# A decoder on one core: FFN, latent text, first preparation and maxima as one list of single steps

## The chip, the cores and the metric

The kernel runs on one core of a Trainium2 chip. The time is the device time of one execution in microseconds (us), lower is better. Three runs of the kernel before took 1716.5, 1719.92 and 1722.71, median 1719.92. All data are float32 unless a line says otherwise.

## What is computed

Six residual blocks run one after another on x of 2 batches x 1024 rows x 256 features:

```python
x = x + linear_attention_and_ffn(layernorm(x))   # stage 1
x = x + latent_cross_attention(ctx, layernorm(x), mask)   # stage 2
x = x + gated_recurrence(layernorm(x))
x = x + causal_attention(layernorm(x))
x = x + cross_attention(layernorm(x), ctx)
x = x + experts(layernorm(x))
```

The change touches stage 1 and the beginning of stage 2:

```python
# stage 1, four heads of 64; b = batch
h = layer_norm(x, ln1)
q = softmax(h @ wq * scale, over 64 features); k = softmax(h @ wk * scale, over rows)
h0 = x + q @ (k.T @ (h @ wv)) @ wo + bo
y = h0 + gelu(layer_norm(h0, ln2) @ w_ff1 + b_ff1) @ w_ff2 + b_ff2
x_out = y @ w_d + b_d
# stage 2, four heads of 64; 64 text keys and the 1024 rows themselves
xn, ln = layernorm(ctx), layernorm(layernorm(x))
q, k, v = ln @ Wq.T, concat(xn, ln) @ Wkv.T ...
out = softmax(mask(rmsnorm(q) * gq / 8 @ rmsnorm(k).T * gk)) @ v @ Wo.T + bo
```

## The kernel before, in words

x stays in SBUF as 16 tiles of 128 rows. Stage 1 works on groups of four tiles (512 rows): groups 0 and 1 are batch 0, groups 2 and 3 batch 1. Stage 2 works by batch; a "unit" is a batch and a pair of heads (units 0 to 3).

Each engine carries out its own instructions strictly in the order in which the program issues them, and waits on semaphores for what other engines produce. Around the change the order is written by hand (`manual_schedule`): the order of the steps in the program is the order of every engine's queue.

**Stage 1** (class Linear, lines 246 to 632) consists of named steps with one engine each. `stat`, `mean`, `norm`, `h0_` are DVE, `root` a power on POOL, `turn` four transposes of 128 x 128 on TensorE into a ps_t tile, `hT` the copy out of it (feature half 0 on DVE, half 1 on ScalarE). `key`, `val`, `query` are eight products each into a ps_s tile; `kmax`, `kneg`, `kexp` and `qmax` to `qdiv` the two softmaxes. `ctx`, `cbd`, `wc`, `wcs` fold k.T v and wo into one matrix per batch; `att`, `radd` add the result to h0. For each group then follow `fstat` to `fT` (second layer norm and turn), eight `up` (two products of 128 x 512 into a ps_t tile) with `gelu` (ScalarE), four `down` (four products into the ps_f tile), `res` (adds h0 by eight products with the identity), `oT` (ScalarE), `last` (eight products into a ps_f tile), `bd` and `ladd` (DVE, into x).

`LINEAR_ORDER` (line 226) lists these steps for the attention of both batches and the FFN of groups 0 and 1, up to the turns of groups 2 and 3. The FFN of groups 2 and 3 is the generator `back` (line 615).

**Stage 2** (class Latent, from line 635) has `text` (line 692), which reads and projects the 128 text rows in few long steps, and `prepare` (line 773), which for one batch takes statistics, a doubled layer norm with two powers on POOL (L144, called from lines 787 and 792), transposes (L808), query-key products in four pieces (L822), squares and copies (ScalarE), sums (L834), a power on POOL (L836), values (L846), scaling (L857) and the transposes of q and k of both head pairs (L867, copied on ScalarE at L870). `start` interleaves `text` and `prepare(0)`; line 2549 interleaves `start` and the two `back` generators, one piece of each in turn.

`maxima(u)` (line 876) finds the largest score of each row of a unit in 18 steps: two text blocks (L886, reduced at L895 and L898) and 16 blocks of 128 rows x 512 keys x 2 heads (L908, reduced by DVE at L915), then a few small DVE operations that split the maxima in three bfloat16 parts (L918 to L925). `augment(u)` turns these for the attention. In `run` (line 1065) all 18 steps of unit 0 and four of unit 1 (LEAD) are issued first, then `attend(0)` follows, with one further max step of unit 1 and one piece of `prepare(1)` per loop step.

PSUM has eight banks. During stage 1 and line 2549 they are two ps_s tiles of two banks, two ps_t tiles of one bank and one ps_f tile of two (`ps_a`, line 2520). From `run` on there are three ps_s tiles, one ps_t and one ps_o (`ps_d`, line 2555). A tile is only written again when its readers are done.

Of the kernel before, what the change touches and what calls it, by code (L numbers as in the profile page):

```python
# [225 lines left out]
LINEAR_ORDER = """  # L226
stat_0 mean_0 stat_1 root_0 mean_1 norm_0 root_1 h0_0 turn_00 turn_01 hT_01 hT_00 norm_1 stat_2 turn_11
turn_10 hT_11 hT_10 h0_1 key_00 stat_3 mean_3 query_00 kmax_00 root_3 kneg_00 mean_2 kexp_00 h0_3 root_2
val_00 qmax_00 qsub_00 bd_0 qexp_00 key_01 vcopy_00 norm_2 qsum_00 qinv_00 qdiv_00 turn_21 turn_20 hT_21
kmax_01 val_01 hT_20 kneg_01 bd_1 kexp_01 kinv_0 qturn_001 norm_3 vcopy_01 qturn_000 qT_001 kturn_00  # L230
qT_000 kturn_01 kr_00 turn_30 kr_01 h0_2 turn_31 query_01 hT_31 hT_30 key_10 qmax_01 qsub_01 qexp_01
ctx_0 qsum_01 qinv_01 qdiv_01 kmax_10 qturn_010 query_10 qT_010 kneg_10 cbd_0 kexp_10 wc_0 qmax_10
qturn_011 wcs_0 val_10 qT_011 qsub_10 qexp_10 qsum_10 att_01 vcopy_10 qinv_10 qdiv_10 qturn_100 radd_01
qturn_101 att_00 qT_101 qT_100 fstat_1 fmean_1 froot_1 key_11 radd_00 fnorm_1 fstat_0 fturn_11 val_11
fmean_0 fT_11 kmax_11 froot_0 kneg_11 fnorm_0 kexp_11 kinv_1 fturn_00 vcopy_11 kturn_10 fT_00 fturn_01
kr_10 kturn_11 fT_01 up_01 kr_11 up_03 gelu_01 up_05 gelu_03 up_02 gelu_05 up_07 gelu_02 up_04 gelu_07
up_00 gelu_04 up_06 gelu_00 down_00 gelu_06 fturn_10 query_11 fT_10 up_12 qmax_11 qsub_11 up_13 gelu_12
qexp_11 down_01 gelu_13 qsum_11 qinv_11 qdiv_11 qturn_111 up_15 qT_111 down_02 gelu_15 up_11 down_03
gelu_11 res_0 up_17 oT_0 up_10 gelu_17 up_16 gelu_10 down_10 gelu_16 down_11 qturn_110 up_14 qT_110
ctx_1 gelu_14 down_12 cbd_1 wc_1 down_13 wcs_1 att_11 res_1 radd_11 fstat_3 att_10 oT_1 fmean_3 froot_3  # L240
fnorm_3 last_1 radd_10 fstat_2 fmean_2 fturn_31 ladd_1 froot_2 fturn_30 fT_31 fT_30 last_0 fnorm_2
fturn_21 ladd_0 fturn_20 fT_21 fT_20
"""


class Linear:
# [355 lines left out]
    def attention(self, own):  # L602

        self.own = own
        self.ksum = own.tile([P, B, DC], F32, tag="ksum", bufs=1, name="ksum")
        self.blocks = []
        for b in range(B):
            c = own.tile([P, DC, P], F32, tag=f"cbd{b}", bufs=1, name=f"cbd{b}")
            self.k.nc.gpsimd.memset(c, 0.0)
            self.blocks.append(c)  # L610
        for step in LINEAR_ORDER.split():
            name, args = step.rsplit("_", 1)
            getattr(self, "h0_" if name == "h0" else name)(*(int(a) for a in args))

    def back(self, g):

        for f2 in range(4):
            for fc in (2 * f2, 2 * f2 + 1):
                self.up(g, fc)
                self.gelu(g, fc)  # L620
            yield
            if f2:
                self.down(g, f2 - 1)
                yield
        self.down(g, 3)
        yield
        self.res(g)
        self.oT(g)
        yield
        self.bd(g)  # L630
        self.last(g)
        self.ladd(g)


class Latent:
# [13 lines left out]
    def __init__(self, k, x, wt, pool):  # L649
# [40 lines left out]
        self.undivided = None  # L690

    def text(self, ctx, mask):

        k, nc, pool, w = self.k, self.k.nc, self.pool, self.w
        tile = lambda name, shape, dt=F32: pool.tile(shape, dt, tag=name, bufs=1, name=name)
        cr = tile("cr", [P, CK])
        nc.sync.dma_start(out=cr, in_=ctx)

        m8 = tile("m8", [P, B * CTX], U8)
        nc.sync.dma_start(out=m8, in_=mask[0].partition_broadcast(P))  # L700
        self.mrow = tile("mrow", [P, B, CTX])
        nc.vector.tensor_copy(self.mrow.rearrange("p b n -> p (b n)"), m8)
        nc.vector.tensor_scalar(self.mrow, self.mrow, 1.0, -NEG, ALU.subtract, ALU.mult)
        c8 = tile("c8", [P, B], U8)
        for hh in range(2):
            for b in range(B):
                nc.sync.dma_start(
                    out=c8[hh * 64 : hh * 64 + 64, b : b + 1],
                    in_=mask[0, b * CTX : (b + 1) * CTX].unsqueeze(1),
                )  # L710
        self.mcol = tile("mcol", [P, B])
        nc.vector.tensor_copy(self.mcol, c8)
        nc.vector.tensor_scalar(self.mcol, self.mcol, 1.0, -NEG, ALU.subtract, ALU.mult)
        self.kbd = tile("kbd", [P, B, 2, 2, CTX])
        self.vbd = tile("vbd", [P, B, 2, 2, 64])
        nc.gpsimd.memset(self.kbd, 0.0)
        nc.gpsimd.memset(self.vbd, 0.0)
        mv, r = k.ln_stats(lambda i: cr, 1)
        nc.vector.tensor_scalar(cr, cr, mv[:, 0, 0:1], r[:, 0:1], ALU.subtract, ALU.mult)
        yield  # L720
        tb = k.t()
        for kc in range(2):
            nc.tensor.transpose(tb[:CP, kc * P : (kc + 1) * P], cr[:, kc * CP : (kc + 1) * CP], k.ident)

        xcT = tile("xcT", [CP, 2, B, 2, CTX])
        for kc in range(2):
            for d in range(2):
                k.affine(
                    xcT[:, kc, :, d, :],
                    tb[:CP, kc * P : (kc + 1) * P].rearrange("p (b n) -> p b n", b=B),  # L730
                    k.vec("ln_x_g", kc, CP), k.vec("ln_x_b", kc, CP), d,
                )
        yield
        for b in range(B):
            tb = k.t()
            for kc in range(2):
                nc.tensor.matmul(
                    tb,
                    lhsT=xcT[:, kc, b].rearrange("p d n -> p (d n)"),
                    rhs=w["ckv"][:CP, kc, :],  # L740
                    start=(kc == 0),
                    stop=(kc == 1),
                )
            kt = pool.tile([P, D], F32, tag="ckt", bufs=2, name="ckt")
            sq = pool.tile([P, D], F32, tag="cksq", bufs=2, name="cksq")
            nc.scalar.copy(kt, tb[:, :D])
            for hh in range(2):
                sl = slice(hh * 64, hh * 64 + 64)
                nc.vector.tensor_copy(
                    self.vbd[sl, b, :, hh, :],  # L750
                    tb[sl, D:].rearrange("p (r h d) -> p r h d", h=2, d=64)[:, :, hh, :],
                )
            yield
            nc.vector.tensor_mul(sq, kt, kt)
            ss = k.small([P, 4], "ss4")
            nc.vector.tensor_reduce(ss, sq.rearrange("p (h d) -> p h d", d=64), AX.X, ALU.add)
            nc.vector.tensor_scalar(ss, ss, 1.0 / 64, 1e-16, ALU.mult, ALU.max)
            ri = k.rsqrt(ss, 4)
            k3 = kt.rearrange("p (h d) -> p h d", d=64)
            nc.vector.tensor_tensor(k3, k3, ri.unsqueeze(2).to_broadcast([P, 4, 64]), ALU.mult)  # L760
            tb = k.t()
            for pr in range(2):
                nc.tensor.transpose(tb[:, pr * P : (pr + 1) * P], kt[:, pr * P : (pr + 1) * P], k.ident)
            for hh in range(2):
                sl = slice(hh * 64, hh * 64 + 64)
                nc.vector.tensor_scalar_mul(
                    self.kbd[sl, b, :, hh, :],
                    tb[sl, : 2 * P].rearrange("p (r d n) -> p r d n", r=2, d=2)[:, :, hh, :],
                    self.gk[sl],
                )  # L770
            yield

    def prepare(self, b):

        k, nc, pool, x, w = self.k, self.k.nc, self.pool, self.x, self.w
        lnT = pool.tile([P, DC, N], F32, tag="lnT", bufs=1, name="lnT")

        st, mv = k.small([P, TB, 6], "pr_st", 1), k.small([P, TB, 2], "pr_mv", 1)
        u, rr, nm = (k.small([P, TB], f"pr_{n}", 1) for n in ("u", "rr", "nm"))
        for i in range(TB):  # L780
            nc.vector.bn_stats(st[:, i, :], x[:, 8 * b + i, :])
            if i == 3:
                yield
        for i in range(TB):
            nc.vector.bn_aggr(mv[:, i, :], st[:, i, :])
        nc.vector.tensor_scalar_add(u, mv[:, :, 1], EPS)
        r = k.rsqrt(u, TB)
        yield
        nc.vector.tensor_mul(u, r, r)
        nc.vector.tensor_mul(u, u, mv[:, :, 1])  # L790
        nc.vector.tensor_scalar_add(u, u, EPS)
        r2 = k.rsqrt(u, TB)
        yield
        nc.vector.tensor_mul(rr, r2, r)
# [262 lines left out]
    def start(self, ctx, mask):  # L1057
# [4 lines left out]
        for _ in zip_longest(prepare, text):  # L1062
            yield
# [1620 lines left out]
```

## Time and profile before

The profiled execution took 1725.12 us, of which the span from the first to the last instruction is 1723.4; the other three runs have a median of 1719.92.

| stretch (us from the start) | what runs | TensorE busy | DVE busy | granted TensorE clock |
|---|---|---|---|---|
| 0 to 50 | loads, attention | 39.06 | 40.28 | 1.00 |
| 50 to 100 | attention, FFN | 50.00 | 22.60 | 1.00 |
| 100 to 150 | FFN of groups 0 and 1 | 49.05 | 8.68 | 1.00 |
| 150 to 200 | FFN of group 2, text, batch 0 | 39.37 | 24.37 | 0.90 |
| 200 to 250 | FFN, preparation of batch 0 | 50.00 | 18.66 | 1.00 |
| 250 to 275 | FFN of group 3 | 24.52 | 3.44 | 1.00 |
| 275 to 300 | maxima of unit 0 | 22.51 | 24.69 | 1.00 |
| 300 to 400 | attention of unit 0, preparation of batch 1 | 94.43 | 56.62 | 0.98 |

A busy time is the union of an engine's instructions in the stretch. The end of a matmul in the trace is modelled, so a TensorE that waits a little between two blocks still counts as busy. The clock is the share of full speed that the throttle granted. Products of float32 leave two records each in the trace.

### The profile page before, as it was taken

Reading aid. Unit: us, or ns where it says so; the run is one execution under the profiler, and the core shown is the slowest. Engines: PE = TensorE matmul, PEld = TensorE weight load, DVE = VectorE, ACT = ScalarE, POOL = GpSimd, SP = SyncE. Lnnn points to the kernel's source line nnn. Section 1 sums busy time; section 2 is a strip of 40 time slices with the busy share of each in tenths; the row PEclk is TensorE's granted clock in tenths of the full one; section 3 lists DMA queues with packets and bytes.
Section 4 is the critical chain, followed back from the end, with each engine's and each line's share of the span. In section 5 each row is a group of like instructions: output and inputs, shape, how many; then the busy total and the mean of one; then the engine's idle time right before and its main releaser. Section 6 shows DMA issues by size and latency. Waiting matters only on the chain.

```text
span 1723.4 us, 21309 instructions
## 1 busy us (share of the span) xinstructions
PE 1647.6 (96%) x8815; PEld 885.6 (51%) x8822; DVE 804.0 (47%) x1454; ACT 522.5 (30%) x876; POOL 319.6 (19%) x376
## 2 busy tenths in 40 slices
PE   7998899999999999999999999989999999999998
PEld 5746454343433447443433443446785664666466
DVE  8514236646654425476676668376531311111322
ACT  2321231432223323235455455423221111111110
POOL 2001140342222301113111011220035000000520
PEclk9999999999999999979999999989899999999999
DMA  5000000000000100100000000080014322232321
GB/s 232 1 1 3 1 0 0 1 1 1 1 1 1 40 1 1 32 1 2 1 2 1 1 1 1 2 273 2 1 68 164 122 84 66 95 122 72 106 64 49
DMA packets 36824, 69.68 MB, mean 40 GB/s; under 512 B 5048, under 2 KB 28152, under 8 KB 36344
## 3 DMA queue, kind: packets, MB, share of 16 engines
q1 hardware_dynamic: 28712, 53.61, 9.3%
q0 software_dynamic: 4608, 11.54, 2.1%
q10 hardware_dynamic: 3408, 3.17, 0.5%
q8 instruction: 70, 1.15, 0.3%
q14 instruction: 26, 0.21, 0.0%
HBM read 54.15 MB, written 14.16 MB: 40 GB/s over the span
## 4 chain that ended last, share of the span: by engine, by line
PE 80%; DVE 11%; issue 5%; ACT 2%; POOL 1%; DMA 0%; ACTq 0%; POOLq 0%; DVEq 0%
PE ps_s L2407 18%; PE ps_o L2434 9%; PE ps_s L1396 8%; PE ps_o L1436 5%; PE ps_s L1020 4%; PE ps_t L1355 4%; PE ps_o L947 3%; PE ps_t L1201 3%; PE ps_t L1471 2%; PE ps_s L908 2%; PE ps_t L539 2%; PE ps_s L822 2%; PE ps_s L381 2%; DVE part L915 1%; PE ps_f L556 1%
## 5 line engine op out<-in xcount | busy, mean ns | idle before, releaser
L2407 PE MATMUL ps_s<-xe,w 128*128 128x512 f32 (+1 forms) x528 | 229.0, 592 | 0.0
L1506 ACT ACTIVATE pT<-ps_t 128x512 f32<-128x512 f32 (+3 forms) x344 | 150.6, 490 | 150.3 <-PE ps_t L1471 148.9
L1396 PE MATMUL ps_s<-kT,qT 32*128 32x512 f32 (+3 forms) x768 | 182.9, 574 | 10.0 <-DVE part L1412 6.2
L1471 PE MATMUL ps_t<-qT,kT 32*128 32x512 f32 (+3 forms) x688 | 185.6, 557 | 2.2 <-ACT pT L1506 2.2
L2422 DVE TENSOR_TENSOR hid<-ga,ps_s 128x512 f32<-128x512 f32 (+2 forms) x99 | 62.0, 628 | 266.4 <-ACT ga L2418 266.3
L2407 PEld LDWEIGHTS ps_s<-xe,w 128*128 128x128 f32 (+1 forms) x528 | 98.0, 187 | 121.3 <-issue 120.0
L2434 PE MATMUL ps_o<-wo,hid 128*128 128x256 f32 (+1 forms) x704 | 153.7, 379 | 0.0
L1412 DVE TENSOR_REDUCE part<-ps_s 128x2 f32<-128x1024 f32 (+3 forms) x128 | 130.6, 1024 | 46.9 <-PE ps_t L1471 38.8
L2434 PEld LDWEIGHTS ps_o<-wo,hid 128*128 128x128 f32 (+1 forms) x704 | 133.2, 190 | 18.6 <-issue 0.5
L2418 ACT ACTIVATE ga<-ps_s 128x512 f32<-128x512 f32 (+2 forms) x99 | 54.4, 550 | 245.3 <-PE ps_s L2407 244.0
L1464 POOL TENSOR_SCALAR_AFFINE_SELECT pT<-pT 128x256 f32<-128x256 f32 x128 | 52.2, 408 | 319.5 <-ACT pT L1506 311.7
L1396 PEld LDWEIGHTS ps_s<-kT,qT 32*128 32x128 f32 x768 | 61.6, 195 | 86.8 <-issue 45.2
L1436 PE MATMUL ps_o<-pT,vr 128*32 128x256 f32 (+4 forms) x1408 | 99.3, 360 | 1.8 <-POOL pT L1464 1.5
L1027 ACT ACTIVATE pT<-ps_s 128x1024 f32<-128x1024 f32 x64 | 65.5, 1024 | 115.6 <-PE ps_s L1020 115.6
L915 DVE TENSOR_REDUCE part<-ps_s 128x2 f32<-128x1024 f32 x64 | 76.4, 1218 | 28.4 <-PE ps_s L908 27.7
L1032 POOL TENSOR_TENSOR acc<-acc,pT 128x1024 f32<-128x1024 f32 x24 | 59.5, 2480 | 152.7 <-ACT pT L1027 148.1
L1404 DVE TENSOR_TENSOR ps_s<-ps_s,causal 128x256 f32<-128x256 f32 x128 | 55.0, 430 | 66.6 <-PE ps_t L1471 44.6
L2407 PE MATMUL ps_s<-xin,w 128*128 128x256 f32 (+3 forms) x264 | 81.7, 471 | 0.5 <-DVE hid L2422 0.5
L1436 PEld LDWEIGHTS ps_o<-pT,vr 128*32 128x32 f32 x1408 | 29.0, 109 | 99.3 <-issue 85.4
L1471 PEld LDWEIGHTS ps_t<-qT,kT 32*128 32x128 f32 x688 | 71.6, 192 | 12.1 <-ACT pT L1506 6.9
L908 PE MATMUL ps_s<-kT,qT 64*128 64x512 f32 x256 | 71.5, 639 | 0.8 <-DVE part L898 0.6
L1020 PE MATMUL ps_s<-qT,kT 64*128 64x512 f32 x256 | 70.2, 625 | 0.2 <-DVE part L915 0.2
(401 smaller groups left out, 2361.8 us busy)
## 6 DMA issues: line engine op xcount, KB each, us to landing
w<-in_w SPq DMA_DIRECT2D x32, 684.0 KB, 8.5
wo<-in_wo SPq DMA_DIRECT2D x8, 1280.0 KB, 7.0
xi_rows<-xin SPq DMA_DIRECT2D x8, 384.0 KB, 8.1
eo_rows<-rows ACTq DMA_DIRECT2D x12, 256.0 KB, 5.5
xr<-xi_rows POOLq DMA_DIRECT2D x48, 64.0 KB, 7.3
w_ffn<-in_w_ffn SPq DMA_DIRECT2D x1, 2304.0 KB, 13.9
x<-in_x SPq DMA_DIRECT2D x4, 512.0 KB, 5.4
w<-in_w_cell SPq DMA_DIRECT2D x2, 1024.0 KB, 16.5
```

The lines of the kernel that those rows point to most:

```text
L908: nc.tensor.matmul(s3[:, hh, :], lhsT=q[rows, qt * P : (qt + 1) * P], rhs=kt[rows, half * 512 : (half + 1) * 512], start=True, stop=True,)
L915: nc.vector.tensor_reduce(part[:, half, qt, :], s3, AX.X, ALU.max, negate=True)
L1020: nc.tensor.matmul(s3[:, hh, :], lhsT=self.ones_h[hr, :] if i else kt[hr, kk * P : (kk + 1) * P], rhs=rows[hr, cols] if i else q[hr, cols] ...
L1027: nc.scalar.activation(pT, s3, AF.Exp)
L1355: nc.tensor.matmul(s, lhsT=self.w[name][:, kc, grp * P : (grp + 1) * P], rhs=self.xT[b][:, kc, cols], start=(kc == 0), stop=(kc == DC - 1),)
L1396: nc.tensor.matmul(s3[:, hh, :n], lhsT=q[rows, qt * P : (qt + 1) * P], rhs=kt[rows, at : at + n], start=True, stop=True,)
L1412: nc.vector.tensor_reduce(out, s3[:, :, :n], AX.X, ALU.max, negate=True)
L1436: nc.tensor.matmul(self.o[hh * 32 : hh * 32 + 32, cols], lhsT=vr[:, kk, 4 * grp + hh, :], rhs=pts[hh // 2][:, hh % 2, cols], start=first, ...
L1471: nc.tensor.matmul(out, lhsT=kt[rows, kk * P : (kk + 1) * P], rhs=q[rows, j * 512 + q0 : (j + 1) * 512], start=True, stop=True,)
L1506: nc.scalar.activation(pT[:, hh, q0:], heads[hh][:, q0:], AF.Exp)
L2407: self.k.nc.tensor.matmul(s[:m, i * 512 : i * 512 + n], lhsT=wt[:, kc, at : at + m], rhs=self.inputs[e][:, kc, first : first + n], start=( ...
L2434: self.k.nc.tensor.matmul(o, lhsT=self.hid[:n, hc, st * P : (st + 1) * P], rhs=self.to[:n, hc, :], start=(hc == 0), stop=(hc == len(HCH) - 1),
```

## The change

1. Stage 1 gets a new order, `FRONT_ORDER`, which goes up to the first turn of group 3; what follows moves to the second list.
2. `text`, `prepare` and `maxima` are taken apart into single steps like those of stage 1 (`tstat` to `tkeys`; `stat` to `kcopy`; `tmax`, `tred`, `max`, `red`, `part`). `prepare` and `maxima` stay, as loops over these steps, for batch 1 and the later units.
3. One list, `JOINT_ORDER`, replaces `back`, `start` and the first 22 max steps: it orders the FFN of groups 2 and 3, the text, the preparation of batch 0, all maxima of unit 0 and four blocks of unit 1 step by step. Names with `l_` are those of Latent; a `'` puts a copy on the other engine. All maxima of unit 0 now use the tiles of `ps_a`.
4. In `prepare`'s steps the doubled layer norm takes one power of v(1+eps)+eps^2 per half batch (width 4) instead of two of width 8, and `scale` works on two tiles of rows at a time instead of four.

```diff
-LINEAR_ORDER = """
...
+FRONT_ORDER = """
+stat_0 mean_0 stat_1 root_0 mean_1 norm_0 root_1 stat_3 turn_01 turn_00 hT_01 norm_1 hT_00 turn_10 hT_10
+turn_11 h0_0 hT_11 query_01 mean_3 bd_0 root_3 stat_2 key_00 qmax_01 norm_3 qsub_01 turn_31 turn_30 hT_31
+kmax_00 key_01 qexp_01 kneg_00 hT_30 kexp_00 qsum_01 qinv_01 qdiv_01 val_00 kmax_01 kneg_01 mean_2 kexp_01
+h0_1 root_2 qturn_010 vcopy_00 qturn_011 bd_1 val_01 qT_011 kinv_0 qT_010 norm_2 h0_2 kturn_01 vcopy_01
+turn_20 kr_01 bd_2 kturn_00 kr_00 turn_21 query_00 hT_21 hT_20 h0_3 bd_3 key_10 qmax_00 qsub_00 qexp_00
+val_11 kmax_10 kneg_10 qsum_00 kexp_10 qinv_00 qdiv_00 ctx_0 vcopy_11 qturn_001 cbd_0 query_11 qT_001 wc_0
+qmax_11 qturn_000 qsub_11 query_10 wcs_0 qexp_11 qT_000 qsum_11 att_00 qmax_10 qsub_10 qinv_11 qexp_10
+qdiv_11 att_01 radd_00 fstat_0 fmean_0 qturn_111 radd_01 froot_0 key_11 qT_111 fnorm_0 fstat_1 fturn_00
+kmax_11 fturn_01 val_10 fT_01 kneg_11 fT_00 kexp_11 fmean_1 qsum_10 froot_1 kinv_1 qinv_10 qdiv_10 up_04
+vcopy_10 fnorm_1 up_05 gelu_04 kturn_11 gelu_05 up_01 kr_11 up_00 gelu_01 up_06 gelu_00 up_02 gelu_06
+down_00 gelu_02 fturn_11 up_03 fT_11 up_07 gelu_03 down_01 gelu_07 qturn_101 qturn_100 qT_101 down_02
+qT_100 down_03 res_0 fturn_10 oT_0 qturn_110 fT_10 kturn_10 qT_110 up_10 kr_10 up_17 gelu_10 up_14 gelu_17
+up_12 gelu_14 up_13 gelu_12 up_15 gelu_13 up_11 gelu_15 last_0 gelu_11 ctx_1 ladd_0 down_10 cbd_1 down_11
+down_12 wc_1 up_16 wcs_1 att_11 gelu_16 down_13 radd_11 fstat_3 fmean_3 att_10 froot_3 fnorm_3 fturn_30
+radd_10
+"""
+
+JOINT_ORDER = """
+fturn_31 res_1 fT_31 fT_30 l_stat_00 up_32 oT_1 l_mean_00 fstat_2 l_root_00 up_31 gelu_32 l_shift_00
+fmean_2 l_norm_00 froot_2 up_30 l_tstat_ l_mask_ l_troot_ gelu_31 fnorm_2 l_bias_00 last_1 gelu_30
+l_tnorm_ up_37 ladd_1 l_stat_01 l_tturn_ gelu_37 down_30 l_txT_1 l_mean_01 l_txT_0 l_root_01 l_shift_01
+l_tprod_1 up_35 l_tvals_1 l_tcopy_1 l_tsum_1 up_34 l_tinv_1 gelu_35 l_tdiv_1 fturn_21 gelu_34 l_turn_00
+fT_21 l_tback_1 l_lnT_001' l_lnT_000' l_tprod_0 l_norm_01 l_tkeys_1 l_val_00 l_tvals_0 l_tcopy_0 l_bias_01
+l_tsum_0 l_tinv_0 l_prod_01 l_vcopy_00 l_tdiv_0 l_turn_01 l_keep_01 l_tback_0 l_square_01 l_lnT_010 up_36
+l_sums_01 l_prod_00 gelu_36 l_tkeys_0 l_inv_01 l_lnT_011' l_prod_03 l_square_00 l_sums_00 l_keep_00
+l_scale_01 l_inv_00 l_prod_02 l_square_03 l_keep_03 l_sums_03 l_inv_03 l_scale_00 up_33 l_square_02
+l_keep_02 l_sums_02 fturn_20 gelu_33 l_val_01 fT_20 l_inv_02 l_scale_03 down_31 l_vcopy_01' l_scale_02
+l_qturn_01 l_kturn_01 l_qcopy_01' up_25 l_kcopy_01 l_kturn_00 gelu_25 l_qturn_00 l_kcopy_00' up_26
+l_qcopy_00 l_max_071 gelu_26 l_tmax_00 l_red_071 up_24 l_tred_00 l_max_040 gelu_24 l_max_001 l_red_040
+up_27 l_red_001 l_max_061 gelu_27 l_max_031 l_red_061 down_32 l_red_031 l_max_021 l_max_051 l_red_021
+down_33 l_red_051 l_max_030 l_max_010 l_red_030 res_3 l_red_010 l_max_011 oT_3 l_tmax_01 l_red_011 last_3
+l_tred_01 l_max_000 ladd_3 l_max_041 up_22 l_red_041 l_red_000 up_20 gelu_22 l_tmax_10 gelu_20 l_max_101
+l_tred_10 up_23 l_red_101 l_max_020 gelu_23 l_max_060 l_red_020 up_21 l_red_060 l_max_070 gelu_21
+l_max_100 l_red_070 down_20 l_red_100 down_21 down_22 down_23 res_2 l_max_050 oT_2 l_tmax_11 l_red_050
+last_2 l_part_0 l_tred_11 ladd_2
+"""
+
+def play(order, *objects):
+    for step in order.split():
+        other = step.endswith("'")
+        name, args = step.rstrip("'").rsplit("_", 1)
+        to = objects[name.startswith("l_")]
+        name = name.removeprefix("l_")
+        getattr(to, "h0_" if name == "h0" else name)(*(int(a) for a in args), *((True,) if other else ()))
...
-        for step in LINEAR_ORDER.split():
-            name, args = step.rsplit("_", 1)
-            getattr(self, "h0_" if name == "h0" else name)(*(int(a) for a in args))
-
-    def back(self, g):
...
+        play(FRONT_ORDER, self)
...
+    def mean(self, b, g):
...
+        v = self.of["v", b, g] = self.small(4, "p_v")
+        nc.vector.tensor_scalar(v, mv[:, :, 1], 1.0 + EPS, EPS * EPS, ALU.mult, ALU.add)
...
+    def root(self, b, g):
+        self.of["r", b, g] = self.k.rsqrt(self.of["v", b, g], 4)
...
+    def prepare(self, b):
+
+        self.stat(b, 0)
+        yield
+        self.stat(b, 1)
+        for g in range(2):
+            self.mean(b, g)
+            self.root(b, g)
+        yield
+        for g in range(2):
+            self.shift(b, g)
+            self.norm(b, g)
+            yield
+            self.turn(b, g)
+            for kc in range(DC):
+                self.lnT(b, g, kc)
+        yield
+        for j in range(TB // 2):
+            for step in (self.prod, self.square, self.keep, self.sums, self.inv):
+                step(b, j)
+            yield
+        for g in range(2):
+            self.val(b, g)
+            self.vcopy(b, g)
+            yield
+        for g in range(2):
+            self.scale(b, 2 * g)
+            self.scale(b, 2 * g + 1)
+            yield
...
-    def start(self, ctx, mask):
...
     def run(self, late, following):
...
-        ahead = iter(())
-        made = 0
+        made = n + self.LEAD
+        ahead = self.maxima(1, self.LEAD)
...
-        for _ in range(n):
-            max_step()
-        for _ in range(2):
-            max_step()
         self.augment(0)
-        for _ in range(self.LEAD - 2):
-            max_step()
...
             with tc.manual_schedule():
-                for _ in zip_longest(chain(linear.back(2), linear.back(3)), start):
-                    pass
+                latent = Latent(k, x, w_lat, early)
+                latent.read(a["ctx"], a["mask"])
+                play(JOINT_ORDER, linear, latent)
```

## The prediction

> **What bounds the kernel now.** I read the page first, then TensorE's (PE's) waits up to 310 us, then the PE timeline and busy time in stretches around each wait, last the VectorE (DVE) timeline there.
>
> ```profile
> PE 1647.6 (96%) x8815; PEld 885.6 (51%) x8822; DVE 804.0 (47%) x1454; ACT 522.5 (30%) x876; POOL 319.6 (19%) x376
> ```
>
> TensorE is busy 96% of the span and carries 80% of the chain that ended last. So only what TensorE waits for can be won, or what makes its clock slow. The change touches the work up to about 400 us. PE's waits there (us in total, times, longest):
>
> ```profile
> PE ps_t L302 <- DVE xh L183: 10.9, 2, 9.8
> PE ps_t L763 <- DVE ckt L760: 5.1, 2, 3.5
> PE ps_f L590 <- DVE x L600: 3.7, 1, 3.7
> PE ps_t L933 <- DVE mparts L923: 1.6, 1, 1.6
> PE ps_t L539 <- DVE hT L134: 1.3, 1, 1.3
> PE ps_t L302 <- DVE qe L434: 0.9, 1, 0.9
> ```
>
> Each is short work of DVE or POOL in front of which nothing else was queued for TensorE. The two long ones cost more than they show (PE timeline: start, us, instruction, [idle before]; then stretches with busy time and PEclk, the granted clock):
>
> ```profile
> 150.59 3.62 PE L590 MATMUL ps_f<-w_ffn,oT 128*128 128x256 f32 x16
> ...
> 158.76 6.45 PE L590 MATMUL ps_f<-w_ffn,oT 128*128 128x256 f32 x16 [3.68 <-DVE x L600]
> ...
> 275.52 15.74 PE L908 MATMUL ps_s<-kT,qT 64*128 64x512 f32 x56 [0.20 <-DVE part L898]
> ```
>
> ```profile
> 160.00:165.00 5.00, 5.00 (x14) 4.01 (x14) 1.38 (x7) 0.00 (x0) 0.56 (x1) 0.57 0.00 0
> 195.00:200.00 5.00, 4.35 (x9) 2.21 (x10) 1.13 (x3) 1.43 (x3) 0.05 (x1) 0.66 0.00 0
> 276.00:292.00 16.00, 15.97 (x62) 4.65 (x59) 16.00 (x15) 0.00 (x0) 0.00 (x0) 1.00 0.00 1
> ```
>
> The same 16 records take 3.62 us at full clock and 6.45 after the 3.68 us wait, at a clock of 0.57. In the last stretch PE looks busy, but DVE is busy for all 16.00 us: it reduces one block of maxima per 1.13 us (18.18 us for 16), and TensorE needs only 0.96 us for a block where nothing holds it (starts 306.51 and 307.47 in the attention loop).
>
> **The change part by part.** Counted in the built programs, TensorE has 5,052 instructions in both; ScalarE loses two table loads; DVE has 4 more, POOL as many. So all gain is lost idle time.
>
> (a) Start. Before, the second product block (`key_00`) ended at 15.24 + 4.75 = 19.99. In the new list DVE goes, from the end of `norm_0` (10.76): `stat_3` 1.32, `norm_1` 1.29, two hT copies of 0.72, which is 14.8; ScalarE's copy `hT_11` (0.78) ends near 15.2; `query_01` takes 3.45 and ends at 18.7. Gain 1.3. Group 3 of x, which `stat_3` now wants at 10.8, was issued at 2.9 and lands within 7.4, at 10.3; the second half of w_lin, which `query_01` wants at 15.2, was issued at 3.73 and lands 8.8 later, at 12.5. Both are in time, the first barely; if late, the gain is 0.
>
> (b) The 0.9 us wait for qe goes: `query_11` now stands ahead of the first gelu, and its exp no longer sits between two table loads of 1.28. Gain 0.9.
>
> (c) End of the linear attention. Before: waits 3.68, 1.25 and 0.56, plus 3.0 of slow clock (6.45 against 3.45 a block), 8.5 in all. In the new list, counted from the end of `att_11`: `radd_11` to `fnorm_3` took 145.55 to 154.08, 8.5 us, of which `fnorm_3` 4.27, because POOL sets up the latent stage's tables at that moment:
>
> ```profile
> 149.81 4.27 DVE L183 TENSOR_SCALAR fxh<-h,f_mv,rs_y 128x256 f32<-128x256 f32 x4 [1.12 <-POOL rs_y L144]
> ```
>
> TensorE's cover is `down_13` 3.43 and `att_10` 3.45, so it waits about 1.8. The rule in the Trainium skill (SBUF — State Buffer, on the shared port pair) is that a DVE operation in a two-port mode and a POOL operation exclude each other for a whole instruction. By the rule alone, a lock that DVE wins each time, `fnorm_3` is the 1.3 that `norm_0` took, and there is no wait; the row says 4.27 in the same neighbourhood, and I take the row. After it, `radd_10` (1.2) and the copy `fT_30` (0.8) end 10.7 after `att_11`, and `up_32` is reached at 11.6 after two turns (0.9) and `res_1` (1.8): no second wait. `last_1` has three up blocks ahead of it, `last_0` has its `ladd_0` far behind. Gain 8.5 - 1.8 = 6.7.
>
> (d) Text. Before: 1.60 + 3.53 of waits for ckt, and 1.4 of slow clock in the two groups behind (0.66 and 4.77 us, against 0.41 and 3.60): 6.5. Now `down_30`, `up_35`, `up_34` and turns stand between `tprod_1` and `tback_1`, and products of 3.4 each ahead of `tback_0`. What can be late is `tnorm`: POOL's `bias_00` (3.1 a piece in the row of L204, now issued early) may hold `fnorm_2` ahead of it for one such instruction; then `ladd_1` frees the ps_f tile about 0.4 after TensorE reaches `down_30`. Gain 6.1. The six reads of text and mask wait on SP for the same engines as before; DVE needs them some 8 us after `att_10`, and they landed in 1.9 to 3.2: hidden, and 0 to 2 us if late.
>
> (e) Maxima of unit 0. From 271.29 to 297.65 (26.4) TensorE did 18 max blocks at 0.96, 4 text blocks at 0.87 (eight 128-column records, as for L867) and the 0.6 of `augment`: 21.4 of work, 5.0 lost. In the new list they go in pairs (1.92) between blocks of at least 1.72: a pair's tiles come back every 3.64 at the soonest, where two reductions take 2.26; no wait. New at the seam: `augment`'s ps_t tile lies where `last_2`'s ps_f tile was, so it waits for `ladd_2` (1.2), 1.3. Gain 5.0 - 1.3 = 3.7. The 0.5 for oT at 267.73 goes too; exp's table load still has time.
>
> (f) Preparation of batch 1, inside the attention loop: one POOL power of width 4 (1.0) per half replaces two in a row of width 8 (1.65 each) with a DVE trip between.
>
> ```profile
> 310.67 2.30 DVE L794 TENSOR_TENSOR pr_rr<-rs_y,rs_y 128x8 f32<-128x8 f32 x1 [0.62 <-POOL rs_y L144]
> ```
>
> This small operation sat out POOL's acc (2.35), and TensorE then waited 2.3 in eight pieces for xh. In the new code the turn comes one loop step earlier, but its norm a whole step ahead of it (about 3.3 of TensorE work against 2.06). Gain 2.0; between 0 and 3. The 2.35 wait for qk (L857) I leave: four 1.22 operations for two of 2.2, one step earlier, may meet another acc; -2 to +2.
>
> **A rule against the change.** The skill (TensorE: Matmul & The Clock Gate, on a second HAM failure mode) says that cycling PSUM tiles with short idles between groups of matmuls can make the clock fall back to half. The new list cycles two ps_s tiles between other products for some 58 us. The row of 276 to 292 is this very case, every block paced by DVE, at a clock of 1.00; by it the cost is 0. By the rule, half of 58 us at half clock would lose 14.5. I take the row: the clock fell behind the waits of 3.68 and 3.53, and somewhat (0.91 from 360 to 380) about the one of 2.35, not among short ones.
>
> **Sum.** 1.3 + 0.9 + 6.7 + 6.1 + 3.7 + 0.5 + 2.0 = 21.2. The list has some hundred handovers that I did not follow one by one, and short ones of 0.16 to 0.56 stand in the PE timeline of before; I take 3 off for them (0 to 9). That leaves 18. The profiled execution took 1725.1 (span 1723.4), which would become 1707; the runs shown have a median of 1719.9, so I predict **1702**. With the bounds above the gain lies between 7 (9 for handovers, (a) and (f) nothing, qk worse by 2) and 24 (no handovers, (f) 3, qk better by 2).
>
> **Rivals.** 1. *The list has waits of its own.* TensorE takes its queue strictly in order, and one short DVE step placed a little early stops everything; for it, the hand-placed list of before shows such waits in the rows above; against it, DVE is busy 47% and TensorE has long blocks to lay over. Half the gain goes: 1711. 2. *The clock falls*, the slower one: short waits in the joint list keep the clock at half. A us at half clock loses half a us, so it passes the gain of 18 from 36 us of half clock on; at 44 us of it: 1724. Against it, the 1.00 above; for it, 0.57 and 0.66 behind two waits, and one new wait at `fturn_30` of about 1.8 in small pieces. 3. *The change is not on the path*: the attention stage behind takes up whatever comes earlier, because its DVE or POOL is late: 1719. Against it, from 396 to 440 TensorE is busy 43.85 of 44.
>
> **Chances.** Forecast 0.76 (its own range 1695 to 1709), rival 1 0.14, rival 2 0.05, rival 3 0.05. This measurement can tell a change from about 0.3%, 5.2 us. Rival 1's spread (1706 to 1717) puts a quarter of it within 0.3%, so: faster 0.87, same 0.08, slower 0.05. The range 1693 to 1714 takes in these bounds (1696 to 1713), most of rival 1, and at its lower end the 3 us by which the runs shown lie from their median.
>
> **What would show it.** In the new profile: no PE wait over 2.5 us after 16 us; `query_01` ending near 18.7; waits for ckt and x gone and PEclk 1.0 throughout 150 to 280; max blocks between up and down blocks; one wait near 1.8 at `fturn_30` and one near 1.3 at `augment`; first xh turn of batch 1 without a wait. A clock below 0.9 in the joint stage, or a wait of several us at one of its turns, would make me wrong.

## The result, and the profile after

The changed kernel takes 1706.24 us (median of 12 runs, 1698.44 to 1713.04), the kernel before 1724.45 (12 runs, 1716.5 to 1726.71, the three shown among them). The ratio is **0.9899, 95% interval 0.9882 to 0.9916**: about 18 us, or 1.0%, faster. Two later measurements gave 0.9908 (0.9874 to 0.9941) and 0.9913 (0.9877 to 0.995). The profiled execution of the changed kernel took 1704.63 us, with a span of 1702.8.

First the page's busy row, then TensorE's waits up to 400 us (us in total, times, longest):

```profile
PE 1636.1 (96%) x8816; PEld 881.5 (52%) x8822; DVE 809.1 (48%) x1458; ACT 515.3 (30%) x870; POOL 310.3 (18%) x376
```

```profile
PE ps_t L333 <- DVE xh L183: 10.5, 2, 9.4
PE ps_s L967 <- DVE qk L937: 4.6, 1, 4.6
PE ps_s L1055 <- DVE part L1046: 0.8, 2, 0.6
PE ps_s L1182 <- DVE part L1065: 0.7, 2, 0.4
PE ps_s L887 <- ACT xh L875: 0.7, 4, 0.2
PE ps_t L333 <- DVE hT L134: 0.2, 1, 0.2
```

The waits for ckt, x, mparts and qe are gone. Of the first row, 9.4 us are the first wait for data, as before. One long wait is new: 4.6 us for qk, where there had been one of 2.4. TensorE has practically as many records as before (8816, 8815); that they took 1636.1 us instead of 1647.6 goes with a mean granted clock of 0.985 instead of 0.976 in these two executions.

To see where the time went I use two landmarks. One is the first product of the attention loop on unit 0 (L1009 before, L1171 after); the other the two text blocks of unit 2 in that loop (L886 before, L1031 after), behind the whole preparation of batch 1. The table also gives TensorE's first matmul, which hangs on the arrival of x, and the rest of the span behind the second landmark.

| us | before | after | difference |
|---|---|---|---|
| first matmul | 9.84 | 9.42 | -0.42 |
| end of the first 24 product records | 23.3 | 25.1 | +1.9 |
| first product of the attention loop | 299.48 | 280.76 | -18.7 |
| text blocks of unit 2 | 388.20 | 372.13 | -16.1 |
| rest of the span | 1335.2 | 1330.7 | -4.5 |

So the change **lost 1.9 us at the start, won 20.6 between 25 and 281, and lost 2.7 in the preparation of batch 1** (88.72 us between the two landmarks before, 91.37 after). The rest of the span is work that it doesn't touch. That rest took 1343.4 and 1325.9 in two further profiles of the same changed kernel, so the 4.5 are not shown to be a gain of the change. The time goes with the mean granted clock here: of the twelve runs of the changed kernel, those at 0.977 and 0.978 took 1711.56 to 1713.04 us, the one at 0.988 took 1698.44.

How the 20.6 us look in the changed kernel: first the end of the linear attention on TensorE (start, us, instruction); then some of the maxima of unit 0, which now come in pairs between blocks of the FFN. The third fence has stretches (us of the stretch; busy time of PE, PEld, DVE, ACT, POOL; granted clock; DMA): one with such maxima in it, and the one behind the new wait.

```profile
149.74 3.62 PE L412 MATMUL ps_s<-wc,qT 128*128 128x256 f32 x16
153.19 1.04 PE L333 MATMUL ps_t<-ident,fxh 128*128 128x128 f32 x8
154.07 1.95 PE L599 MATMUL ps_f<-ident,h 128*128 128x128 f32 x16
155.85 5.32 PE L570 MATMUL ps_t<-hT,w_ffn 128*128 128x512 f32 x12
161.01 1.24 PE L621 MATMUL ps_f<-w_ffn,oT 128*128 128x256 f32 x5
```

```profile
252.19 1.99 PE L1055 MATMUL ps_s<-kT,qT 64*128 64x512 f32 x8
254.11 1.98 PE L570 MATMUL ps_t<-hT,w_ffn 128*128 128x512 f32 x4
256.02 1.99 PE L1055 MATMUL ps_s<-kT,qT 64*128 64x512 f32 x8
```

```profile
250.00:275.00 25.00, 25.00 (x80) 11.26 (x79) 6.73 (x8) 2.61 (x4) 0.00 (x0) 1.00 0.00 1
355.00:365.00 10.00, 8.62 (x30) 3.05 (x30) 4.45 (x10) 4.02 (x4) 4.29 (x2) 0.66 0.01 2
```

No TensorE row carries a bracket with an idle time, and each group takes what it takes at full clock: a pair of maxima 1.99 us, where DVE's pace had made it 2.26. From 250 to 275 TensorE counts as busy throughout, DVE for 6.73 of 25 us: the reductions run beside the FFN.

### The profile page after: what moved, and what is told of

Its sections match the earlier page's. It is cut to its first block, busy times and chain, and to the rows that moved or that the text cites. A ratio compares the mean times of both kernels' runs of the same rounds, so it can differ in the third digit from the quotient of the medians.

```text
span 1702.8 us, 21329 instructions
## 1 busy us (share of the span) xinstructions
PE 1636.1 (96%) x8816; PEld 881.5 (52%) x8822; DVE 809.1 (48%) x1458; ACT 515.3 (30%) x870; POOL 310.3 (18%) x376
## 4 chain that ended last, share of the span: by engine, by line
PE 87%; DVE 9%; ACT 2%; issue 1%; POOL 1%; DMA 0%; SPq 0%; ACTq 0%; POOLq 0%; DVEq 0%
PE ps_s L2556 18%; PE ps_o L2583 9%; PE ps_s L1545 8%; PE ps_o L1585 5%; PE ps_s L1182 4%; PE ps_t L1504 4%; PE ps_s L1055 3%; PE ps_t L570 3%; PE ps_f L587 3%; PE ps_o L1109 3%; PE ps_t L1350 3%; PE ps_s L412 3%; PE ps_t L1620 2%; PE ps_s L904 2%; PE ps_t L1693 1%; DVE part L1561 1%
## 5 line engine op out<-in xcount | busy, mean ns | idle before, releaser
L1545 PE MATMUL ps_s<-kT,qT 32*128 32x512 f32 (+3 forms) x768 | 178.2, 553 | 11.2 <-DVE part L1561 7.2
L1620 PE MATMUL ps_t<-qT,kT 32*128 32x512 f32 (+3 forms) x688 | 182.0, 547 | 2.2 <-ACT pT L1655 2.2
L2583 PEld LDWEIGHTS ps_o<-wo,hid 128*128 128x128 f32 (+1 forms) x704 | 133.2, 190 | 18.6 <-issue 0.5
L1109 PE MATMUL ps_o<-pT,vr 128*64 128x512 f32 x256 | 69.5, 624 | 0.9
```

The costliest lines, as they stand in the source:

```text
L1109: nc.tensor.matmul(self.o[hh * 64 : hh * 64 + 64, :], lhsT=self.vr[b][:, kk, h * 64 : (h + 1) * 64], rhs=pT[:, hh, :], start=first, stop=last,
L1545: nc.tensor.matmul(s3[:, hh, :n], lhsT=q[rows, qt * P : (qt + 1) * P], rhs=kt[rows, at : at + n], start=True, stop=True,)
L1620: nc.tensor.matmul(out, lhsT=kt[rows, kk * P : (kk + 1) * P], rhs=q[rows, j * 512 + q0 : (j + 1) * 512], start=True, stop=True,)
L2583: self.k.nc.tensor.matmul(o, lhsT=self.hid[:n, hc, st * P : (st + 1) * P], rhs=self.to[:n, hc, :], start=(hc == 0), stop=(hc == len(HCH) - 1),
```

## The experiments

They were made in three sets, each on one chip with its own runs of the kernel before; the chip of the first set is slower (before: 1750.64 us), the others not (1723.59 and 1722.63). Ratios are to the kernel before on the same chip.

| kernel | median us | ratio and 95% interval | loop's first product | text blocks of unit 2 |
|---|---|---|---|---|
| *first set* | | | | |
| ri4: four buffers for p_ri | 1732.32 | 0.9905 (0.9871, 0.9939) | 280.8 | 365.23 |
| warm: dummy transposes first | 1734.29 | 0.9919 (0.989, 0.9947) | 280.1 | 370.46 |
| both: warm and ri4 | 1725.0 | 0.9865 (0.983, 0.9901) | 280.5 | 364.96 |
| max_out: maxima out of the list | 1746.13 | 0.9971 (0.9954, 0.9988) | 287.7 | 379.42 |
| *second set* | | | | |
| after_copy: the changed kernel | 1709.6 | 0.9908 (0.9874, 0.9941) | 279.5 | 370.24 |
| warm2: dummy transposes, elsewhere | 1713.24 | 0.9945 (0.992, 0.9969) | 281.2 | 372.67 |
| both2: warm2 and ri4 | 1704.17 | 0.99 (0.9869, 0.9931) | 283.0 | 367.24 |
| front_only: the new front alone | 1723.33 | 1.0006 (0.9988, 1.0025) | 301.0 | 389.80 |
| *third set* | | | | |
| after_again: the changed kernel | 1705.54 | 0.9913 (0.9877, 0.995) | 280.1 | 371.09 |
| joint_only: the joint list alone | 1716.4 | 0.9946 (0.9929, 0.9964) | 282.3 | 374.18 |
| old_start: old first 22 steps | 1712.45 | 0.9932 (0.9906, 0.9958) | 283.7 | 375.27 |
| start_ri4: old_start and ri4 | 1701.79 | 0.9874 (0.9838, 0.9911) | 282.4 | 366.82 |

### The new wait: two buffers for the inverse roots

In the changed kernel POOL's powers (L931), DVE's scalings (L937) and the turns behind them (L967) stand like this; one fence for each engine's timeline:

```profile
345.88 6.62 POOL L931 TENSOR_TENSOR p_ri<-p_ss,minus_half 128x16 f32<-128x16 f32 x2 [26.64 <-DVE qk L937]
```

```profile
349.65 1.23 DVE L937 TENSOR_TENSOR qk<-qk,p_ri 128x1024 f32<-128x1024 f32 x1 [1.65 <-POOL p_ri L931]
352.52 3.35 DVE L937 TENSOR_TENSOR qk<-qk,p_ri 128x1024 f32<-128x1024 f32 x1 [1.64 <-POOL p_ri L931]
```

```profile
355.93 0.69 PE L967 MATMUL ps_s<-ident,qk 128*128 128x128 f32 x2 [4.55 <-DVE qk L937]
357.07 2.08 PE L1182 MATMUL ps_s<-qT,kT 64*128 64x512 f32 x4 [0.45 <-DVE part L1065]
```

The bracket of the first line is the reading: POOL stood 26.64 us until DVE had used an earlier `qk`. A power writes p_ri and reads p_ss; it doesn't need qk. So it waited for a *buffer*: p_ri comes from `small`, which has two, and the third power overwrites the first, which the first scaling has to have read. In before, the roots of all four pieces were one tile, `ri`. The products behind then ran at half clock (2.08 us for a group that takes 1.13). The last scaling adds to the wait: it took 3.35 us where the one ahead of it took 1.23, and it began 0.06 us after an `acc` of POOL (2.33 us from 352.46). The edit:

```diff
-        ri = self.of["ri", b, j] = self.small(16, "p_ri")
+        ri = self.of["ri", b, j] = self.pool.tile([P, 16], F32, tag="p_ri", bufs=4, name="p_ri")
```

> The changed kernel with four p_ri tiles instead of two, so that no power on POOL waits for a scaling on DVE. Theory (buffer rotation): the changed kernel's 4.6 us wait of TensorE for qk in the attention of unit 0, and the half clock behind it (about 2.5 us), come from powers 2 and 3 waiting for scalings 0 and 1; the two powers then start right behind their sums, the wait falls below 1 us, the kernel is 5 to 7 us faster than the changed one, ratio to before 0.986. Rival (DVE is full there, or POOL's acc holds the port): powers come early, but the scalings still end late; wait 3 us or more, ratio 0.989 to 0.990.

In ri4 the third and fourth powers run at once (POOL), and the turns hardly wait (TensorE):

```profile
320.87 2.90 POOL L931 TENSOR_TENSOR p_ri<-p_ss,minus_half 128x16 f32<-128x16 f32 x1 [1.25 <-DVE p_ss L927]
327.56 2.90 POOL L931 TENSOR_TENSOR p_ri<-p_ss,minus_half 128x16 f32<-128x16 f32 x1 [3.80 <-DVE p_ss L927]
```

```profile
351.45 0.44 PE L967 MATMUL ps_s<-ident,qk 128*128 128x128 f32 x2 [0.24 <-DVE qk L937]
```

With the loop starting at the same 280.8, the text blocks come at 365.23 instead of 372.13: **6.9 us**, of which 4.3 are the wait and the rest slow clock. A scaling still meets an `acc` in ri4 (two of them take 3.48 us together); what the buffers remove is the late start. From the loop's first product to the text blocks it is 84.2 to 84.5 us in the four kernels with four buffers, and 90.4 to 91.9 in the eight with two. Pairs that differ in this edit alone differ there by 6.9 (ri4, and the changed kernel on another chip), 5.9 (both, warm), 7.2 (both2, warm2) and 7.2 (start_ri4, old_start).

The totals say less. ri4's ratio of 0.9905 is what the rival expected, and the changed kernel did not run in that set. In the other three pairs the medians differ by 9.3, 9.1 and 10.7 us, more than the landmarks; the surplus is not shown to be of the edit.

### The start: half clock

TensorE's start in before, in the changed kernel, and in old_start, which is described below:

```profile
13.23 2.21 PE L302 MATMUL ps_t<-ident,xh 128*128 128x128 f32 x8 [1.10 <-DVE xh L183]
15.24 4.75 PE L351 MATMUL ps_s<-hT,w_lin 128*128 128x512 f32 x8
19.83 4.48 PE L381 MATMUL ps_s<-w_lin,hT 128*128 128x256 f32 x20
```

```profile
14.41 1.12 PE L333 MATMUL ps_t<-ident,xh 128*128 128x128 f32 x4 [0.24 <-DVE hT L134]
15.32 6.55 PE L412 MATMUL ps_s<-w_lin,hT 128*128 128x256 f32 x16
21.71 2.74 PE L382 MATMUL ps_s<-hT,w_lin 128*128 128x512 f32 x6
```

```profile
15.34 4.60 PE L381 MATMUL ps_s<-hT,w_lin 128*128 128x512 f32 x8
19.78 3.62 PE L411 MATMUL ps_s<-w_lin,hT 128*128 128x256 f32 x16
25.12 1.64 PE L332 MATMUL ps_t<-ident,xh 128*128 128x128 f32 x8 [1.73 <-DVE xh L183]
27.22 5.37 PE L381 MATMUL ps_s<-hT,w_lin 128*128 128x512 f32 x8 [0.46 <-DVE qe L446]
```

A product block takes 3.6 us once the clock is up. If a block's surplus over 3.6 is half of the time that it ran at half speed (an estimate), full speed came at about 17.5 us in before and at about 21 in the changed kernel. In the latter TensorE has new breaks at 14.41 and, for the copy hT on ScalarE, ahead of a weight load at 16.40 (0.74).

**warm** and **warm2** tried to bring the clock up by dummy transposes into a PSUM tile that nothing reads. The first has 24 of them ahead of everything; the second spreads them between the turns as well.

```diff
+        tb = self.k.t()
+        for i in range(24):
+            at = i % 4 * P
+            self.k.nc.tensor.transpose(tb[:, at : at + P], self.k.ident, self.k.ident)
         play(FRONT_ORDER, self)
```

> The changed kernel with 24 transposes of the identity on TensorE before the first step, their output read by nobody. Theory (cold clock): query_01 took 6.4 instead of 3.45 us because TensorE was still at half clock until about 21 us; with work from 2 us on it runs at full clock, query_01 takes 3.5, and the kernel is about 3 us faster, ratio 0.988. Rival (late operand: the hT_11 copy or the weight DMA, or load traffic): query_01 still needs over 6 us, ratio 0.990 or slower by what the 24 transposes delay the first turn.

```diff
+    def warm(self, n):
+        for i in range(n):
+            at = i % 8 * P
+            self.k.nc.tensor.transpose(self.of["warm"][:, at : at + P], self.k.ident, self.k.ident)
...
-        play(FRONT_ORDER, self)
+        self.of["warm"] = self.k.f()
+        play(7 * "warm_8 " + FRONT_ORDER.replace("hT_01 norm_1", "warm_7 warm_7 hT_01 norm_1").replace("turn_11 h0_0", "warm_8 turn_11 h0_0"), self)
```

> The changed kernel with idle transposes that keep TensorE busy until the first turn, between turn_00 and turn_10 and ahead of turn_11, in the ps_f tile so that the turns' ps_t tiles do not shift. Theory (cold clock): query_01 takes 3.5 to 4.3 us, key_00 begins near 19.5 instead of 21.7, 2 us off the kernel. Rival (query_01 is slow for another reason): key_00 begins at 21.5 or later.

Neither gained. In warm the query block took 4.27 us, but began at 16.91, since its turns now waited 2.80 for a ps_t tile; the first 24 records ended at 24.5. In warm2 the query block ran from 16.49 to 20.65, so it was short as expected but began about a microsecond late; the 24 records ended at 24.1, against 23.9 in after_copy on the same chip. The shorter blocks fit a slow clock as the cause of the 6.55 us. Both kernels with four p_ri buffers:

> Both edits. If both theories hold, 8 to 10 us faster than the changed kernel, ratio to before 0.984; if neither, 0.990.

> warm2 with four p_ri tiles. Against the changed kernel of this set 2 us by the warm start and 7 us by the tiles: ratio to before 0.985, the two text blocks of unit 2 begin near 363 instead of 372. If the clock in the later stages takes part of it back, the ratio is 0.987 to 0.988 though that mark is the same.

The ratios were 0.9865 and 0.99: the gain of the buffers came (5.9 and 7.2 us, above), that of the dummy transposes did not. In both2 the 24 records ended as late as 25.9.

**old_start** puts the order of before back for 22 steps, up to `key_00 stat_3 mean_3`.

```diff
-stat_0 mean_0 stat_1 root_0 mean_1 norm_0 root_1 stat_3 turn_01 turn_00 hT_01 norm_1 hT_00 turn_10 hT_10
-turn_11 h0_0 hT_11 query_01 mean_3 bd_0 root_3 stat_2 key_00 qmax_01 ...
+stat_0 mean_0 stat_1 root_0 mean_1 norm_0 root_1 h0_0 turn_00 turn_01 hT_01 hT_00 norm_1 stat_2 turn_11
+turn_10 hT_11 hT_10 h0_1 key_00 stat_3 mean_3 query_01 bd_0 root_3 qmax_01 ...
```

> Only the first 22 steps are put back into the order of before (both halves of the turns first, then the key product of block 0, then the query product). Theory: the half clock at the start lasts until TensorE has worked some 4 us without a break, and the changed order puts two breaks there (0.24 us ahead of the second turn and 0.7 us ahead of the third load of weights, both for copies of hT). Then the key and query products of the first two blocks together (24 records) end at 23 us or earlier instead of 24.3 to 25, and the whole linear attention is 1 to 3 us earlier, so the maxima L1171 come at 277.5 to 279. Rival: the half clock ends at about the same time whatever the order (a fixed time from the first matmul), then nothing moves by more than 0.5 us at the start.

Its first 24 records ended at 23.2 us against 24.5 in after_again. One such pair says little, since the changed kernel's own profiles lie between 23.9 and 25.1. Counted from the first matmul to the end of the 24 records, the four profiles with the old order (before, joint_only, old_start, start_ri4) took 12.8 to 14.3 us, six with the new order (the changed kernel three times, ri4, max_out, front_only) 14.4 to 15.7. So the order matters, by 1.8 us in the mean. That the breaks are the reason is not shown: the new order also starts with the other block. In old_start the turn of group 3 waited 1.73 us for xh, whose `stat_3` now came 6.4 us later on DVE, and the block behind took 5.37 at a clock that had fallen again. The loop's first product came at 283.7, where 277.5 to 279 was expected and after_again has 280.1. The early `stat_3`, which looked like the cause of the slow start, paid for itself 10 us later. **start_ri4** has this start with four buffers:

> The old first 22 steps, and four buffers for the inverse roots of the preparation (p_ri). If both losses are real and add up, the wait at L967 falls from 4.5 us to under 0.5 us, the unit-2 text blocks come 7 us earlier than in the changed kernel plus what old_start shows (362 to 365 us), and the median is 7 to 10 us under the changed kernel's on this chip (ratio to before 0.984 to 0.987). Rival: the clock dips of the later stages take it back, then the landmark moves but the median only by 0 to 4 us.

The text blocks came 8.5 us earlier than in old_start (1.3 of it already at the loop's first product) and 4.3 earlier than in after_again, at 366.82 where 362 to 365 was expected, since old_start loses. Its median is the lowest of its set, 3.8 us under after_again's, but the intervals of the two overlap.

How long the half clock lasts is not settled, and it varies without any change of the program. By the estimate above, full speed came 3.1 (joint_only), 4.0 (old_start), 4.3 (before) and 5.9 us (start_ri4) after the wait that ended at about 13 us, with the same order of TensorE's first blocks. With the new order it came at 18.6, 19.7 and 21.2 us in three profiles of the same kernel.

### Which part of the change holds the gain

**max_out** issues all maxima of unit 0 and four blocks of unit 1 ahead of the attention loop, as before, and has the rest of the change.

```diff
-        made = n + self.LEAD
-        ahead = self.maxima(1, self.LEAD)
+        made = 0
+        ahead = iter(())
...
+        for _ in range(n + 2):
+            max_step()
         self.augment(0)
+        for _ in range(self.LEAD - 2):
+            max_step()
```

> The changed kernel with the maxima of unit 0 and the four lead blocks taken out of the joint list and issued in front of the attention loop, as before the change. Theory (TensorE idle under DVE's pace): they cost 5 us more than in the list, the attention loop begins about 5 us later against the changed kernel's 279.7, ratio 0.993. Rival (the list's own order or the fewer operations made the gain, the place of the maxima is worth nothing): loop begins within 1 us, ratio 0.990.

TensorE in max_out:

```profile
255.91 3.72 PE L616 MATMUL ps_f<-w_ffn,oT 128*128 128x256 f32 x16 [1.36 <-ACT oT L603]
...
263.70 15.74 PE L1050 MATMUL ps_s<-kT,qT 64*128 64x512 f32 x56 [0.20 <-DVE part L1041]
...
283.29 0.62 PE L1090 MATMUL ps_t<-ident_h,mparts 128*128 128x128 bf16 x8 [1.55 <-DVE mparts L1070]
```

DVE's pace is back (15.74 us for 56 records, as before), and so is the wait for mparts. The loop begins 6.9 us later than in the changed kernel (about 5 was expected). Of this, 2.7 are two waits for oT, one of them shown: without the maxima the FFN's last steps have nothing to cover ScalarE's copy.

**front_only** is the kernel before with the new order of the linear attention (steps that the new order leaves to the joint list stand at its end, in their old order).

> The kernel before with the new front order, its missing last steps in the old order behind it, and the old back, start and maxima. Theory (the gain is in the joint list: covers for the text, the second norm chain and the maxima): the front order alone gives the 0.9 us of the qe wait and loses some 2 us at the start, so the attention loop begins within 2 us of before's 297.8 and the ratio is 0.998 to 1.001. Rival (the new front order is where the gain is): the loop begins 8 us or more earlier, ratio 0.995.

No gain, as expected: 1.0006, and its landmarks are 1.5 us later than in before. It still has the long waits, and in it fnorm_3 takes 4.26 us.

**joint_only** is the reverse: the old order of the linear attention to its end, then the joint list without those steps; `bd_2` and `bd_3` come ahead of `last_2` and `last_3`.

> The linear attention is played to its end in the old order, and only then the joint list (without those steps; the two block-diagonal copies of the context come ahead of the last two products). If a third of the gain is the end of the linear attention laid beside the text stage (8.5 us of waits at the turns of the FFN's input and of the latent text in before), the first maxima of the attention loop (L1171) come 6 to 8 us later than in the changed kernel, about 286 to 288 us, and the total is 5 to 8 us longer (1712 to 1716). Rival: the joint list alone holds the gain, since the waits at the end of the linear attention are taken up by the list's later slack; then the maxima come within 2 us of the changed kernel, or earlier by up to 2 us because the old start is quicker.

The first product of the loop comes at 282.3, 2.2 us later than in after_again and not 6 to 8: nearer to the rival. (Its start is quicker: the first 24 records ended at 22.8 us against 24.5. So the steps that the new order moves are worth nearer 4 us, an estimate from these two differences; 0.9 of it is the wait for qe, which is back.) The medians of the two kernels differ by 10.9 us, far more than the landmarks, but their runs had different clocks: at 0.976 eleven runs of joint_only took 1715.3 to 1717.7 us, and the one of after_again took 1715.49.

Yet in joint_only nothing of the end of the linear attention is laid beside the text stage. Its TensorE there (before had idle times of 3.68, 1.25 and 0.56, and 6.45 us for the first of these groups):

```profile
155.03 3.72 PE L620 MATMUL ps_f<-w_ffn,oT 128*128 128x256 f32 x16 [0.44 <-DVE x L630]
158.58 1.04 PE L332 MATMUL ps_t<-ident,fxh 128*128 128x128 f32 x8
160.11 5.42 PE L569 MATMUL ps_t<-hT,w_ffn 128*128 128x512 f32 x12 [0.49 <-ACT hT L136]
166.55 1.98 PE L569 MATMUL ps_t<-hT,w_ffn 128*128 128x512 f32 x4 [1.03 <-ACT fT L579]
```

About 6 of the 8.5 us go although no step of TensorE was moved there. What differs is seen on DVE: from the start of `fnorm_3` to that of `ladd_1`, for which TensorE waited, it needed 7.71 us in before and 4.43 in joint_only. Of these 3.3 us, 2.9 are `fnorm_3` itself; the rest are small steps of the text that stood in between. The first two fences are `fnorm_3` in joint_only and in the changed kernel (in before it took 4.27 us from 149.81). The others are POOL's large memset in joint_only, in the changed kernel and in before, and the last memset of before's run:

```profile
149.32 1.38 DVE L183 TENSOR_SCALAR fxh<-h,f_mv,rs_y 128x256 f32<-128x256 f32 x4 [1.12 <-POOL rs_y L144]
```

```profile
150.77 1.38 DVE L183 TENSOR_SCALAR fxh<-h,f_mv,rs_y 128x256 f32<-128x256 f32 x4 [1.12 <-POOL rs_y L144]
```

```profile
151.02 1.84 POOL L680 MEMSET mparts<- 128x1024 bf16 x2
```

```profile
152.47 1.84 POOL L681 MEMSET mparts<- 128x1024 bf16 x2
```

```profile
151.04 1.85 POOL L671 MEMSET mparts<- 128x1024 bf16 x2
153.41 0.53 POOL L716 MEMSET kbd<- 128x512 f32 x1
```

In before the large memset began 1.23 us after the start of `fnorm_3`. The last of the norm's four pieces (some 0.4 us each) had just begun, at 150.9. It took 3.21 us and ended at 154.08, when POOL's run of memsets was over (153.94). In joint_only the memset began 1.70 us after the norm's start, when all four had ended. The same split shows in all five: 1.23 and a norm of 4.27 or 4.26 in before and front_only; 1.70 and 1.38 in joint_only, the changed kernel and after_again.

The lines that set up these tables are unchanged. But they now stand inside `manual_schedule`, so POOL takes the small ones (pair, pair1h, ones_h, ident_h) in the order of their lines; before it was another order. Ahead of the large memset they take 1.79 us in joint_only and 1.32 in before. So about 2.9 us of TensorE's longest wait seem to have hung on half a microsecond on POOL, as a side effect of the change. This is read from five profiles that agree; no run moved the memset alone.

## Why the prediction was right

The forecast was a gain of 18 us; the medians differ by 18.2. (The time came out at 1706.24 instead of 1702, since the kernel before has a median of 1724.45 over twelve runs instead of 1719.92 over three.) Part of that agreement is luck: errors of opposite sign nearly met, and at the second landmark, ahead of the scatter of the later stages, three profiles of the changed kernel are 16.1, 18.0 and 17.1 us ahead of the one profile of before. Of the signs named in advance, two failed: a wait over 2.5 us came (4.55), and `query_01` ended near 21.7 instead of 18.7. The two waits that were announced did not come. By steps:

**(a) Start: wrong.** Expected +1.3, measured -1.9. `query_01` began at 15.32, as worked out (15.2), but I gave it the 3.45 us of a full clock, and it took 6.55 (5.21 and 5.67 in the two other profiles). I had read the clock column, which says 1.00 there, instead of the row beside it: before's first block took 4.75. The false step is the cost of a product block at the start.

**(b) Wait for qe: right.** It is gone; it is back in joint_only with 0.9, where the old order is.

**(c) End of the linear attention: size about right, reason largely wrong.** All of the 8.5 us went, where I expected 6.7, and no wait arose at `fturn_30`. I took `fnorm_3` at the 4.27 of the row, and it took 1.38: I did not ask which instruction of POOL had made it long, and whether that would still stand there. The 1.3 that I had worked out from the rule of the Trainium skill (SBUF — State Buffer, on the shared port pair) was nearer, but the traces do not confirm the rule. The page speaks of a loser that is blocked for one whole instruction. In before a piece of the norm stood through a run of POOL's instructions (3.21 us), and in the changed kernel all four pieces ran beside its small memsets and casts (150.69 to 152.30) without delay. joint_only shows that most of the gain, about 6 us, comes without laying the steps of TensorE side by side.

**(d) Text: right.** No wait for ckt is left; the clock is 1.00 from 150 to 280. Slow clock behind the waits was counted in the sum, and had to be.

**(e) Maxima: right, the new wait not.** I put the gain at 3.7 with a wait of 1.3 at `augment`; there is none, so 5.0, plus 0.5 for oT. max_out gives 6.9 for taking them out, 2.7 of it in oT waits, a cover that I had counted with only 0.5; that leaves 4.2 for the maxima. The rule of the Trainium skill on a second failure of the clock gate (TensorE: Matmul & The Clock Gate) did not show: two tiles were cycled at a clock of 1.00. With TensorE busy throughout, the list gave it few short idles to act on. (That half of the 58 us would run slow was my assumption; the page gives no share.)

**(f) Preparation of batch 1: half wrong.** The xh turn's waits fell from 2.3 to 0.7, as expected. But the wait for qk, which I bounded at -2 to +2, rose from 2.4 to 4.6 with slow clock behind it, so that the stretch lost 2.7 us instead of gaining 2.0. I had priced the scalings as instructions and overlooked that their inputs had turned from one tile into four turns of a ring of two. That is the false step here, and the only one that made a new long wait; ri4 shows it.

**Handovers: next to none.** The terms (b) to (e), with the two expected waits left out, make 0.9 + 8.5 + 6.1 + 5.0 + 0.5 = 21.0; measured between 25 and 281 are 20.6. The two waits that did not come (3.1 us) and the 3 us taken off for handovers pay for most of the 3.2 us missed in (a) and the 4.7 in (f).

Rival 1 (the list has waits of its own) is excluded for the list, though the one new wait is of this kind; it is in the code behind it. Rival 2 is excluded by the clock, rival 3 by the landmarks.

What stays open: how long the half clock lasts at the start; what sets the clock of the untouched stages, which took 1326 us in a run with a mean clock of 0.988 and 1343 in one with 0.975; and whether the order of POOL's small instructions alone is worth what (c) puts down to it. It wasn't tried to run ri4 beside the changed kernel on one chip.

## What to carry to other kernels

When a step is cut into smaller ones, look at every tile that passes between the pieces: where one tile becomes several in a ring, an engine far ahead now waits for the slowest reader (26.64 us of POOL here, 4.55 of TensorE), and one wider ring undoes it. When a row is longer than its kind (4.27 against 1.38), first find the instruction of the other engine that overlaps it, and ask whether it will still stand there after the change. Where a list is reordered, count the slow clock as well as the idle time, and take the early rows, not the clock column, for what a product costs at the start.

## What was not expected of the hardware

The clock column reads 1.00 before the first recorded change of the clock, although products run at half speed: 1.00 for 16 to 18 us in the changed kernel, within the block that took 6.55. In warm, where TensorE worked from 1.52 to 5.75 us and then stood 4.05, the same column reads 0.50 from 8 to 18 us and 0.98 from 18 to 20.

One piece of a DVE norm that met a POOL memset took 3.21 us instead of 0.4, longer than the whole memset (1.85 for two tiles). It ended 0.14 us after the run of memsets that followed.
